# A graph attention kernel: the row writes issued from ScalarE's DMA queue

## The chip, the cores and the metric

The kernel runs on one core of a Trainium2 chip. A core has five engines, each with an instruction stream of its own that is worked through in order: TensorE (PE), VectorE (DVE), ScalarE (ACT), GpSimd (POOL) and SyncE (SP). Data moves between HBM and the core's memory by DMA; a DMA is an instruction in the stream of the engine that issues it, here SP's nearly always and ACT's for a few weights at the start. The metric is the time of one execution on the device, in microseconds (us), as the median of several runs.

## The reference

Two graph attention blocks are applied to 64 graphs of 256 nodes with 512 features each, in float32. In each block the input goes through a layer norm and a ReLU, the attention network is applied, and the result is added to the input:

```python
def gat_layer(x, mask, W, a_src, a_dst, bias, concat):
    xl = (x @ W).reshape(B, N, H, F)
    asrc = jnp.einsum('bnhf,hf->bnh', xl, a_src)
    adst = jnp.einsum('bnhf,hf->bnh', xl, a_dst)
    e = jax.nn.leaky_relu(asrc[:, :, None, :] + adst[:, None, :, :], NEG_SLOPE)
    e = jnp.where(mask[..., None], e, NEG_INF)
    attn = jax.nn.softmax(e, axis=1)
    out = jnp.einsum('bsdh,bshf->bdhf', attn, xl)
    ...
    return out + bias
```

The first block has two such layers: layer 1 with four heads of 256 features and an ELU after it, and layer 2 with one head of 512. The second block has one attention layer of the same kind, called layer 3 here: eight heads of 64 features, the softmax over the other index, and a ReLU on the output.

## The kernel before, in words

Every graph is worked on as two halves of 128 nodes (`T` = 2, `P` = 128 partitions). The work on three graphs is interleaved: a round of the list `order` has steps of the graph whose layer 3 ends (-2), of the one in layers 2 and 3 (-1), of the one in layers 1 and 2 (0), and of the next one, which is loaded and projected (1). Rounds r = 1 to 63 run through `order`; a list `head` stands before them and `tail` after. The lists are written out by hand, and the program does not reorder them: each step appends its instructions to the streams of the engines in the order of the list. So the order within one engine's stream is that of the list.

Projections are matrix products by Strassen's scheme in the class `Product`: seven products p1 to p7, of which four add onto one PSUM tile `sum`, and in between ACT copies the sum's state away (`kept`, L60). PE can only add the next product onto `sum` once ACT has made the copy. `m1a` and `m1b` are the two halves of layer 1's projection, `m2` and `m3` those of layers 2 and 3; what they give is added up by DVE (L260) or copied by ACT (L258).

The softmax is without a maximum: exponentials of the nodes' terms are taken once per node (`exp1`, `exp2`, `exp3`; ACT at L284 and L481), and an edge is the larger of two products of these. For that one factor is needed along the partitions and the other along the free axis. The step that brings it there is `spread` (called by `rows1`, `rows2` and `rows3`, once each per graph):

- DVE transposes 32x32 blocks of the exponentials into `wt` (L237);
- a DMA of 16 KB writes them to a DRAM tile `kept4`, `kept1` or `kept8` (L239);
- one to four DMAs read this tile back, broadcast to all 128 partitions (`bc`, L244). Four are for layer 3, one for layer 2, two for layer 1. They wait until the write has landed.

For the last graph, layers 2 and 3 use the tensor engine instead. The edges (`weigh`) are then two instructions for each half of a head: ACT scales the row (`wy`, L289; three buffers) and DVE takes the larger and applies the mask (`e`, L290). `gat1`, `gat2` and `gat3` (L394, L448, L500) multiply the edges with the features on PE, and `out1`, `out2`, `out3` bring the result out on DVE. After layer 2 come the statistics of the norm (DVE L173 to L179, GpSimd L181 and L183), the norm (ACT L189) and its transpose on PE (`turn3`, L196).

The part of `order` around the three uses of `spread`:

```python
    -1 exp3, -1 rows3, 1 turn1, 0 m2 p6, 0 m2 p5, 0 m2 p7, ...
    0 exp2, 0 rows2, 1 m1a p6, -1 edges3 0, -1 edges3 1, 1 m1b p1, 1 m1a p7, ...
    ... -1 edges3 3, 1 m1a p4, 1 m1b p2, 1 exp1, 1 rows1, -1
    edges3 6, 1 m1b p6, 1 m1b p5
```

After that the next round begins with `edges3 7`, `gat3 0 0`, `edges3 5`, `gat3 0 1`, `edges2`, `m1b p7`, `out3`, `gat2 0`.

A second path with a general softmax is in the program and is entered only when an exponential runs out of range; it does nothing on these inputs.

Of the kernel before, what the change touches and what calls it, by code (L numbers as in the profile page):

```python
# [97 lines left out]
def short_path(ctx, tc, flags, x, adj, w1, att_src1, att_dst1, b1, w2, att_src2, att_dst2, b2, w_proj, w_att,  # L98
               b_att, out):

    nc = tc.nc
# [131 lines left out]
    def spread(w, heads):  # L233


        wt = small.tile([P, 32], F32, name="wt")
        nc.vector.transpose(wt, w)  # L237
        kept = dram.tile([4, 32, 32], F32, name=f"kept{heads}")
        nc.sync.dma_start(kept.rearrange("j c i -> (j c) i"), wt)  # L239
        rows = []  # L240
        for h in range(0, heads, 2):
            k = min(2, heads)
            bc = work.tile([P, 4, T * k, 32], F32, name=f"bc{k}", bufs=3 * k - 2)
            nc.sync.dma_start(bc.rearrange("p j c i -> p j (c i)"),  # L244
                              kept[:, T * h:T * (h + k), :].rearrange("j c i -> j (c i)")[None].to_broadcast([P, 4, 32 * T * k]))
            rows += [bc[:, :, T * i:T * (i + 1), :].rearrange("p j t i -> p t j i") for i in range(k)]
        return rows
# [44 lines left out]
    class Graph:  # L292
# [87 lines left out]
        def rows1(self):  # L380
            self.bc1 = spread(self.w[0], H1)
# [48 lines left out]
        def rows2(self):  # L430
            self.bc2 = None if self.b == B - 1 else spread(self.w[1], 1)
# [51 lines left out]
        def rows3(self):  # L483
            self.bc3 = None if self.b == B - 1 else spread(self.w[2], H3)
# [27 lines left out]
        def range(self):  # L512
            nc.vector.tensor_reduce(ends[:, 0, self.b:self.b + 1], self.exs, AX.X, ALU.max)
            nc.vector.tensor_reduce(ends[:, 1, self.b:self.b + 1], self.exs, AX.X, ALU.min)
# [434 lines left out]
```

## Time and profile before

| | |
|---|---|
| Time, median of 3 runs | 3218.84 us (3214.32 to 3219.35) |
| Profiled execution | 3218.9 us, of which the span from first to last instruction is 3217.2 us |
| PE busy, of the span | 97% |
| DVE, ACT, POOL busy | 71%, 60%, 37% |
| Granted clock of PE, mean | 0.993 |
| Row writes (L239) | 190, 16 KB each, all issued from SP, 1.4 us to landing |
| Broadcast reads of rows (L244) | 380 of 256 KB (5.7 us to landing) and 63 of 128 KB (4.8 us) |

The profile is one execution of the program. A busy share is the time in which an engine executed something. In the timeline each line has the start, the duration, the engine, the source line, the operation, the tiles written and read, and in brackets how long the engine had idled before and what ended that; lines of one kind that follow each other are merged (x3). SPq and ACTq are instructions that the engine's sequencer works on itself, such as the issue of a DMA. A list of waits has the total in us, the number of times and the longest.

### The profile page before, as it was taken

The numbers are of one execution on the slowest core, as the hardware profiler recorded it, in microseconds if no ns is written. First come the engines' busy times: TensorE is split into PE (matmuls) and PEld (weight loads), VectorE is DVE, ScalarE is ACT, GpSimd is POOL, SyncE is SP. The second block draws the span as 40 slices with busy tenths as digits, with TensorE's granted clock in tenths as the row PEclk, the third lists the DMA queues.
The fourth block names the chain that finished last, engine by engine and source line by source line (L and its number), as shares of the span: only waits on it lengthen the run. The fifth ranks groups of instructions, "written<-read, shape, count | busy, mean of one in ns | idle before, by whom it ended". The sixth has DMA issues, their size and how long they took to land. (4 is left out here: it accounts for less than half of the span.)

```text
span 3217.2 us, 60904 instructions
## 1 busy us (share of the span) xinstructions
PE 3133.7 (97%) x21808; PEld 2670.7 (83%) x21808; DVE 2282.5 (71%) x6379; ACT 1917.4 (60%) x4867; POOL 1179.1 (37%) x1434
## 2 busy tenths in 40 slices
PE   4999999999999999999999999999999999999997
PEld 3788888888888888888888888888888888888886
DVE  7667677677677677676676776776776776776765
ACT  2456566656666665665565566566666666655654
POOL 2343343333433433433433433434434334334332
PEclk8999999999999999999999999999999999999999
DMA  4233333333333333333333333332333333333331
GB/s 143 57 95 83 89 88 91 83 91 87 89 87 92 88 86 84 96 81 90 97 80 90 88 89 83 91 92 83 92 87 88 88 91 88 81 89 96 81 90 35
DMA packets 439842, 281.49 MB, mean 87 GB/s; under 512 B 109168, under 2 KB 389744, under 8 KB 439536
## 3 DMA queue, kind: packets, MB, share of 16 engines
q1 hardware_dynamic: 438160, 275.43, 31.9%
q8 instruction: 177, 2.90, 0.4%
q10 hardware_dynamic: 1376, 2.10, 0.2%
q14 instruction: 129, 1.06, 0.1%
HBM read 199.36 MB, written 69.70 MB: 84 GB/s over the span
## 5 line engine op out<-in xcount | busy, mean ns | idle before, releaser
L289 ACT ACTIVATE wy<-bc,exs_sb 128x256 f32<-128x256 f32 x1646 | 706.9, 498 | 176.1 <-DMA bc<-kept 129.3
L260 DVE TENSOR_TENSOR xl<-pm,kept 128x256 f32<-128x256 f32 (+2 forms) x768 | 321.5, 419 | 285.8 <-PE pm L54 208.7
L510 POOL TENSOR_TENSOR x<-x,o 128x256 f32<-128x256 f32 x256 | 181.1, 728 | 916.0 <-DVE r L506 884.4
L394 PE MATMUL pm<-xl,e 128*128 128x257 f32 x2048 | 489.9, 386 | 17.6 <-DVE e L290 13.6
L290 DVE SCALAR_TENSOR_TENSOR e<-wy,exs_sb,cap 128x256 f32<-128x256 f32 x1024 | 435.8, 478 | 92.4 <-ACT wy L289 92.4
L54 PE MATMUL sum<-w_sb,h1s 128*128 128x257 f32 x2048 | 489.0, 381 | 9.3 <-POOL h1s L216 7.0
L60 ACT ACTIVATE kept<-sum 128x264 f32<-128x264 f32 (+3 forms) x768 | 276.5, 376 | 341.9 <-PE sum L54 336.6
L54 PEld LDWEIGHTS sum<-w_sb,h1s 128*128 128x128 f32 x2048 | 389.3, 190 | 68.7 <-POOL h1s L216 7.2
L394 PEld LDWEIGHTS pm<-xl,e 128*128 128x128 f32 x2048 | 374.3, 190 | 84.0 <-DVE e L290 14.9
L54 PE MATMUL pm<-w_sb,h1s 128*128 128x257 f32 x1536 | 371.1, 383 | 10.4 <-DVE xl L260 6.5
L54 PEld LDWEIGHTS pm<-w_sb,h1s 128*128 128x128 f32 x1536 | 287.0, 190 | 74.9 <-POOL hs L216 20.1
L181 POOL TENSOR_TENSOR rstd<-ve,neg_half 128x2 f32<-128x2 f32 x128 | 117.6, 919 | 630.3 <-DVE ve L179 630.3
L500 PEld LDWEIGHTS pm<-xl,e 128*64 128x64 f32 x8192 | 251.0, 138 | 45.4 <-DVE e L290 23.4
L54 PE MATMUL sum<-w1a_sb,hs 128*128 128x260 f32 x1024 | 269.6, 386 | 11.7 <-ACT kept L60 4.5
L290 DVE SCALAR_TENSOR_TENSOR e<-wy,exs_sb,mask 128x256 f32<-128x256 f32 x640 | 270.3, 480 | 13.1 <-ACT wy L289 12.8
L54 PE MATMUL sum<-w1b_sb,hs 128*128 128x256 f32 x1024 | 271.9, 388 | 2.9 <-ACT hs L353 1.5
L500 PE MATMUL pm<-xl,e 128*64 128x65 f32 x8192 | 270.1, 224 | 2.1 <-DVE e L290 1.3
L54 PE MATMUL sum<-wp_sb,hs 128*128 128x264 f32 x1024 | 270.8, 387 | 1.3 <-ACT kept L60 1.1
L407 ACT ACTIVATE ez<-z 128x512 f32<-128x512 f32 x256 | 159.6, 623 | 178.5 <-DVE z L404 178.5
L404 DVE SCALAR_TENSOR_TENSOR z<-pm,r,b_sb 128x256 f32<-128x256 f32 x512 | 247.8, 484 | 18.3
L448 PE MATMUL pm<-xl,e 128*128 128x257 f32 (+1 forms) x1024 | 242.9, 380 | 1.1 <-DVE e L290 1.1
L54 PEld LDWEIGHTS sum<-w1a_sb,hs 128*128 128x128 f32 x1024 | 191.4, 190 | 50.2 <-issue 15.2
(99 smaller groups left out, 5013.4 us busy)
## 6 DMA issues: line engine op xcount, KB each, us to landing
bc<-kept SPq DMA_DIRECT2D x380, 256.0 KB, 5.7
xs<-in_x_dram SPq DMA_DIRECT2D x64, 512.0 KB, 3.9
out_dram<-x SPq DMA_DIRECT2D x64, 512.0 KB, 2.8
kept_h<-h SPq DMA_DIRECT2D x63, 512.0 KB, 3.2
h<-kept_h SPq DMA_DIRECT2D x63, 512.0 KB, 3.7
ad<-in_adj_dram SPq DMA_DIRECT2D x64, 256.0 KB, 4.3
bc<-kept SPq DMA_DIRECT2D x63, 128.0 KB, 4.8
kept<-wt SPq DMA_DIRECT2D x190, 16.0 KB, 1.4
```

What stands on the lines that cost most here:

```text
L54: self.nc.tensor.matmul(to[:, :self.n], self.lhs[:, i, c, :], self.rhs[:, i, c, :], start=(first and c == 0), stop=(last and c == self.nk ...
L60: self.nc.scalar.activation(s[:, :self.n], self.sum[:, :self.n], AF.Copy)
L181: nc.gpsimd.tensor_tensor(rstd, ve[:, 0, :], neg_half, ALU.pow)
L260: nc.vector.tensor_tensor(dst, pm, add, ALU.add)
L289: nc.scalar.activation(wy.rearrange("p (t j i) -> p t j i", t=T, j=4), bc, AF.Copy, scale=yw)
L290: nc.vector.scalar_tensor_tensor(dst, wy, xw, mask, ALU.max, op)
L394: nc.tensor.matmul(pm[:, :Q + 1], self.e[1, h][:, s, t * P:(t + 1) * P], xl1[:, s, h, L1:], start=(s == 0), stop=(s == T - 1))
L404: nc.vector.scalar_tensor_tensor(z[:, sl], pm[:, :Q], r, b1_sb[:, sl], ALU.mult, ALU.add)
L407: nc.scalar.activation(ez, z[:, 2 * g * F1:2 * (g + 1) * F1], AF.Relu, scale=-1.0)
L448: nc.tensor.matmul(pm[:, :n], self.e[2][:, s, t * P:(t + 1) * P], xl2[:, s, half, L2:L2 + n], start=(s == 0), stop=(s == T - 1))
L500: nc.tensor.matmul(pv[q:q + 64, h, :], self.e[3, a * G + h][:, s, t * P + q:t * P + q + 64], xl3[:, s, a * G + h, :], start=(s == 0), stop ...
L510: nc.gpsimd.tensor_tensor(to, to, o.rearrange("p h k -> p (h k)"), ALU.add)
```

## The change

The write of the transposed row to DRAM is issued by ScalarE instead of SyncE. Nothing else is changed. It applies to all three uses, rows1, rows2 and rows3, and to 190 DMAs in the program. In ACT's stream the write stands right behind the three exponentials of its layer and ahead of the instruction that followed them: a copy of `sum` (L60) after layers 2 and 3, and the `wy` of edges3 6 (L289) after layer 1. In SP's stream the reads of `bc` now follow what stood ahead of the write. The streams of PE, DVE and GpSimd are the same as before.

```diff
@@ -236,7 +236,7 @@
         wt = small.tile([P, 32], F32, name="wt")
         nc.vector.transpose(wt, w)
         kept = dram.tile([4, 32, 32], F32, name=f"kept{heads}")
-        nc.sync.dma_start(kept.rearrange("j c i -> (j c) i"), wt)
+        nc.scalar.dma_start(kept.rearrange("j c i -> (j c) i"), wt)
         rows = []
         for h in range(0, heads, 2):
             k = min(2, heads)
```

## The prediction

> **What bounds the kernel now.** I read the page's first part, then windows over one steady graph, SP's own waits, and last the timelines around the three row writes.
>
> The page's first part (engine, busy us, share of the span):
>
> ```profile
> PE 3133.7 (97%) x21808; PEld 2670.7 (83%) x21808; DVE 2282.5 (71%) x6379; ACT 1917.4 (60%) x4867; POOL 1179.1 (37%) x1434
> ```
>
> TensorE is the bound. Busy time by windows in the steady part:
>
> ```profile
> 1000.00:1048.85 48.85, 48.70 (x345) 41.78 (x344) 34.94 (x97) 30.20 (x77) 18.17 (x22) 1.00 0.31 89
> ...
> 1036.00:1048.00 12.00, 12.00 (x111) 10.22 (x109) 11.40 (x36) 6.55 (x14) 3.25 (x6) 1.00 0.36 106
> ```
>
> The columns are length, PE, PEld, DVE, ACT, POOL. A graph takes about 48.85 us and PE is busy 48.70 of it, at full clock (1.00). PE has no slack, so whatever makes it wait is added to the time. ACT has 18 us free per graph, but what counts is whether it is free where its results are due. In the second window DVE is busy 11.40 of 12.00 us: there it can hardly catch up.
>
> SP's waits (total us, times, longest):
>
> ```profile
> SPq L239 <- DVE wt L237: 560.9, 129, 23.7
> SPq L239 <- DVE e L290: 331.6, 61, 5.9
> ...
> SPq L244 <- DMA kept<-wt: 214.7, 190, 2.9
> ```
>
> SP stands 892 us at the row write until VectorE has transposed the row. SP has nothing else to do, so that cost nothing. After the change somebody else stands there. The three places in one graph, in the timeline (start, us, engine, line). First the rows of layer 1, the last of the three:
>
> ```profile
> 1030.13 0.44 ACT L284 ACTIVATE exs_sb<-xl 128x8 f32<-128x8 f32 x3
> ...
> 1030.48 0.89 ACT L289 ACTIVATE wy<-bc,exs_sb 128x256 f32<-128x256 f32 x2
> ...
> 1031.05 0.20 DVE L237 STREAM_TRANSPOSE wt<-exs_sb 128x32 f32<-128x32 f32 x1
> ...
> 1031.28 0.33 SPq L239 DMA_DIRECT2D kept<-wt  x1
> ...
> 1031.57 0.38 ACT L60 ACTIVATE kept<-sum 128x256 f32<-128x256 f32 x1 [0.20 <-PE sum L54]
> 1031.85 2.49 ACT L289 ACTIVATE wy<-bc,exs_sb 128x256 f32<-128x256 f32 x6
> ...
> 1033.98 0.88 DVE L290 SCALAR_TENSOR_TENSOR e<-wy,exs_sb,mask 128x256 f32<-128x256 f32 x2
> ```
>
> ACT finishes the exponentials at 1030.57, but DVE reaches the transpose only at 1031.05, behind its queue of edges; SP issues at 1031.28. ACT meanwhile goes on with eight wy. Second, the row of layer 2:
>
> ```profile
> 1023.96 0.44 ACT L284 ACTIVATE exs_sb<-xl 128x2 f32<-128x2 f32 x3
> ...
> 1024.43 0.33 SPq L239 DMA_DIRECT2D kept<-wt  x1
> 1024.55 0.39 ACT L60 ACTIVATE kept<-sum 128x260 f32<-128x260 f32 x1 [0.16 <-PE sum L54]
> ...
> 1025.22 0.60 PE L54 MATMUL sum<-w1a_sb,hs 128*128 128x260 f32 x2
> ```
>
> The matmuls at 1025.22 add onto the sum which the copy (L60) must have read; it is read by 1024.94. Third, the point where the chain comes back to PE (turn3):
>
> ```profile
> 1046.49 1.52 ACT L189 ACTIVATE h<-x,off,rstd 128x512 f32<-128x512 f32 x2 [0.78 <-POOL off L183]
> ...
> 1048.06 0.31 PEld L196 LDWEIGHTS pt<-ident,h 128*128 128x128 f32 x3 [0.16 <-ACT h L189]
> ```
>
> h is ready at 1048.01 and the weight load starts 0.05 us later, having waited 0.16; the matmuls over it (1047.97 on) just lose nothing. The chain DVE, GpSimd, ACT into turn3 has no slack left.
>
> **What the Trainium skill says.** "DMA: Bandwidth & Descriptors", section "Issuing engines are not separate DMA queues": transfers from any engine run on the same 16 DMA engines, and another issuer saves only sequencer time. So the 16 KB write itself gains nothing; its landing stays 1.4 us in this trace. "Perfetto Trace Analysis", section "DMA Instruction — HWDGE (DVE, Sync)": the sequencer itself does the semaphore wait and the descriptor generation, and is free for the next instruction only at the end of the profiled window. The section "DVE / Act Engine Instruction (TENSOR_ADD, Activation, etc)" there says that an ACTIVATE's wait sits in a queue beside the sequencer. So a waiting DMA holds up every later ACTIVATE. The trace agrees as far as it goes: at the start two ACT issues run from 12.38 to 14.12 and the next ACTIVATE starts at 14.17, 0.05 after. The skill's section "SWDGE vs HWDGE vs iDMA" of the DMA page says that an issue from ACT is of the same kind as one from SP; here a 256 KB w1a issue takes 374 ns on ACT and 368 on SP, so I take SP's 0.33 us for the kept write on ACT.
>
> **The change part by part.** All 190 writes (64 of layer 1, 63 each of layers 2 and 3) leave SP and come into ACT's stream right behind the exponentials. On PE, DVE and GpSimd no instruction moves. On SP the next instruction is the bc load, which waits for the write to land (1.4 us) as before; 0.33 us of SP's issue per write is saved on an idle queue: nothing.
>
> *Layer 3's row.* DVE has the row transposed at 1015.41 and ACT's last exponential ends at 1015.64, so ACT does not wait; it issues until 1015.97 at the latest, and the copy behind it (1015.55 before) runs from 1016.02 to 1016.39. The sum that it reads is wanted by PE at 1016.99, and ACT's next copy idles 3.0 us for PE. Cost 0; these 0.6 us on PE's side are the cover. Without them: 0.3 to 0.5 us each.
>
> *Layer 2's row.* DVE is quick here (transposed at 1024.40), so ACT issues 1024.43 to 1024.76, the copy starts at 1024.81 instead of 1024.55 and ends at 1025.20. In this graph PE starts 0.14 us after such a release (at 1019.92, after DVE's 1019.78) and the first eight matmuls then take 1.98 instead of 1.90. So PE goes on at 1025.34 instead of 1025.22: 0.12 + 0.08 = 0.20 us. In 16 of 61 steady graphs the records have PE itself over 0.05 us later at this sum, which hides part of the delay; I take 0.16 on average.
>
> *Layer 1's rows.* ACT waits until 1031.28, issues to 1031.61, goes on at 1031.66 instead of 1030.48: 1.18 us late. Queued behind: two wy, the copy, six wy, whose consumers are DVE's edges. The wy start 0.40 apart, so the copy would have been ready at 1031.28 but waited for PE until 1031.57: 0.29 comes back. The last wy ends 0.89 late, and so do the layer 2 edges (L290 with mask, 1034.86 to 1035.75), as DVE was waiting for ACT. PE's gat2 loads its first edge weights at 1035.10 and wants the first half, now at 1035.35: 0.3 us of stall. DVE stays 0.89 late through out3 and out2; at the second L458 it had been waiting for PE (1036.65 to 1037.73 for two, where 0.88 is needed): 0.20 comes back. From there to the statistics of layer 3 DVE has no gap, so h reaches turn3 0.89 - 0.20 = 0.69 us late against a slack of zero. PE's total per graph is the 0.69 (the 0.3 at gat2 lies within it), on top of layer 2's 0.16.
>
> *Sum.* The place occurs in the 62 rounds that have a next graph: 62 x (0.69 + 0.16) = 53 us, and about 2 for refilling PE after a stall. The head's writes are covered (ACT idles 9.0 us there for bc). Profiled execution: 3218.9 (span 3217.2) + 55 = 3274. The median of the runs is 3218.84, the same, so I forecast 3273.
>
> *Ends of the unknown price.* No row shows an ACT issue in the steady part. If it took ACT no time and only the wait counted: layer 2 nothing, layer 1 0.85 - 0.29 - 0.20 = 0.36, 22 us. At the longest ACT issue of the trace (0.545): 0.2 more at both places, 1.27 per graph, 79 us. Below nothing is excluded for ACT's part: no work leaves it.
>
> **The rivals.**
> Absorbed further on (+7 to +30 us, about 3237): DVE or ACT finds slack before turn3 that I haven't seen. For: ACT idles 1.82 us for bc later in the round. Against: it is DVE that is late then, and DVE is full.
> Unchanged (3219): a waiting DMA doesn't hold up the ACTIVATEs behind it. For: the trace has no ACT issue that waits for DVE. Against: the order at the start.
> Faster (3201 at best): on a ring of its own the row write lands earlier, bc arrives earlier, and ACT's waits for bc (129.3 us in 54) shrink. PE idles 5.6 us in 1000, so all its stalls are worth 18 us. It decides only if the write's 1.4 us falls by more than ACT's 1.18 us of delay; nothing queues ahead of the write on SP's ring at those moments.
> A larger loss (above +80, about 3315): the late DVE also holds PSUM buffers which gat2 and gat1 want, and the stalls add up instead of lying within each other.
>
> **How the numbers follow.** The forecast 0.65; absorbed 0.16; larger 0.09; unchanged 0.06; faster 0.04. A measurement tells about 0.2% (6.4 us) from no change. Slower is 0.65 + 0.16 + 0.09 = 0.90, same 0.06, faster 0.04. The range from +18 to +87, 3237 to 3306, holds the forecast case with both ends of the issue's price, half of the absorbed case and a little of the larger one, about 8 in 10.
>
> **What would show it.** In the changed profile: the kept write as an ACT issue of about 0.33 us; the period at 49.7 us; ACT idle some 0.7 to 1.1 us before wy in each graph with the DMA issue in it; DVE waiting longer for ACT's wy; new waits of PE's weight loads for DVE's e at L448 and for ACT's h at L196, and of PE's sum for ACT's L60. I am wrong if ACT's next instruction starts before the write's issue has ended, if h at turn3 is no later against PE than now, or if the bc loads land more than 0.3 us earlier.

## The result, and the profile after

| | before | after |
|---|---|---|
| Time, median (runs side by side on one chip, 4 each) | 3216.58 us (3213.99 to 3219.35) | 3259.88 us (3257.87 to 3260.22) |
| Ratio, 95% interval | | 1.0133 (1.0120 to 1.0145) |
| Span of the profiled execution | 3217.2 us | 3258.3 us |
| Granted clock of PE, mean | 0.993 | 0.993 |
| Row writes, issue | 332 ns on SP | 326 ns on ACT |
| Row writes, to landing | 1.4 us | 1.4 us |
| Start of one gat2 to the next, median of the steady rounds | 48.58 us | 49.36 us |

The change costs 43.3 us, 0.70 us for each of the 62 rounds that have a next graph. The forecast was 3273, 54 us more. The writes are no cheaper from ACT, and no earlier: in the median a row of layer 1 lands 1.45 us after its transposing has ended, before 1.44. The median round grew by 0.78 us, more than the 0.70 that the times give; where the difference goes is told under "Absorbed further on".

The page's first part for the changed kernel (engine, busy us, share of the span, instructions):

```profile
PE 3178.6 (98%) x21808; PEld 2651.7 (81%) x21808; DVE 2280.4 (70%) x6379; ACT 1929.8 (59%) x4867; POOL 1179.6 (36%) x1434
```

Its busy time by windows, the first from gat2 to gat2 (length, then PE, PEld, DVE, ACT, POOL):

```profile
1047.34:1096.70 49.36, 49.21 (x341) 41.08 (x340) 34.92 (x98) 30.09 (x76) 18.18 (x22) 1.00 0.30 88
```

A reader who looks for idle time of PE finds none: its busy time *grew* by 44.9 us with the same 21808 matmuls, and it is busy 49.21 of 49.36 us. In these records the time in which matmuls wait lies inside the matmuls: eight of them at gat2 take 2.22 us where they took 1.89, as shown below. The loss shows in three other places: in the period, in the busy share of the weight loads (81% of the span, 83% before), and in the mean length of one matmul. The group of gat2's matmuls, page of before and then of after (total us, mean ns of one):

```profile
L448 PE MATMUL pm<-xl,e 128*128 128x257 f32 (+1 forms) x1024 | 242.9, 380 | 1.1 <-DVE e L290 1.1
```

```profile
L448 PE MATMUL pm<-xl,e 128*128 128x257 f32 (+1 forms) x1024 | 264.4, 392 | 1.5 <-DVE e L290 1.1
```

The waits of the changed kernel (engine, what it wanted, from whom; total us, times, longest):

```profile
DVE e L290 <- ACT wy L289: 158.0, 192, 4.2
ACT wy L289 <- DVE wt L237: 67.2, 62, 1.1
PEld pm L448 <- PE pm L448: 22.6, 62, 0.7
PEld pm L448 <- DVE e L290: 21.9, 63, 1.5
PEld pm L394 <- issue: 20.0, 59, 0.4
PEld pt L196 <- ACT h L189: 15.5, 66, 2.3
```

ACT now stands 1.08 us (67.2 / 62) in every round at the instruction behind the write. DVE waits for ACT's wy 158.0 us (105.2 before). Weight loads of gat2 wait for DVE's edges 63 times (once before), and for gat2's own matmuls 62 times. Loads of gat1 (L394) waited 10.8 us before. The wait for h at turn3 (L196) is the same 15.5 us in 66 as before.

The rows of layer 1 in the timeline, ACT and then DVE (start, us, in brackets the idle time before and what ended it):

```profile
1042.07 0.44 ACT L284 ACTIVATE exs_sb<-xl 128x8 f32<-128x8 f32 x3
1043.22 0.33 ACTq L239 DMA_DIRECT2D kept<-wt  x1
1043.60 0.91 ACT L289 ACTIVATE wy<-bc,exs_sb 128x256 f32<-128x256 f32 x2 [1.08 <-DVE wt L237]
1044.41 0.36 ACT L60 ACTIVATE kept<-sum 128x256 f32<-128x256 f32 x1
```

```profile
1042.99 0.20 DVE L237 STREAM_TRANSPOSE wt<-exs_sb 128x32 f32<-128x32 f32 x1
1044.14 0.89 DVE L290 SCALAR_TENSOR_TENSOR e<-wy,exs_sb,cap 128x256 f32<-128x256 f32 x2 [0.95 <-ACT wy L289]
```

The exponentials end at 1042.51, the transposed row is there at 1043.19, the issue runs from 1043.22 to 1043.55, and wy starts 0.05 us later. Before, wy started 0.35 us after the first exponential, now 1.53. The copy (L60) follows wy at once; before it had waited for PE. DVE, which had no gap there before, now waits 0.95 us.

The row of layer 2 in a round where PE doesn't come late itself:

```profile
1134.43 0.44 ACT L284 ACTIVATE exs_sb<-xl 128x2 f32<-128x2 f32 x3
...
1134.90 0.33 ACTq L239 DMA_DIRECT2D kept<-wt  x1
1135.28 0.39 ACT L60 ACTIVATE kept<-sum 128x260 f32<-128x260 f32 x1 [0.41 <-PE sum L54]
...
1135.78 0.74 PEld L54 LDWEIGHTS sum<-w1a_sb,hs 128*128 128x128 f32 x4 [0.33 <-issue]
```

The copy starts 0.85 us after the first exponential (0.59 before) and ends at 1135.67; PE's next weight load starts 0.11 later and has waited 0.33 (0.08 in the median before). The view names no releaser here, but the load starts 0.11 us after the end of this copy in both kernels, whenever the copy comes.

Where PE takes the delay of layer 1, first at gat2. The eight matmuls before:

```profile
1035.31 1.89 PE L448 MATMUL pm<-xl,e 128*128 128x257 f32 x8
```

And after, with the edges and the load ahead of them:

```profile
1046.81 0.88 DVE L290 SCALAR_TENSOR_TENSOR e<-wy,exs_sb,mask 128x256 f32<-128x256 f32 x2
...
1047.34 0.73 PEld L448 LDWEIGHTS pm<-xl,e 128*128 128x128 f32 x4 [0.33 <-DVE e L290]
1047.34 2.22 PE L448 MATMUL pm<-xl,e 128*128 128x257 f32 x8
```

The first half of the edges is there at about 1047.29, the load starts 0.05 later, and the eight matmuls take 2.22 us where they took 1.89. Then at gat1, ahead of turn3. Before:

```profile
1045.59 0.42 DVE L508 SCALAR_TENSOR_TENSOR o<-pm,r 128x256 f32<-128x256 f32 x1
...
1046.13 0.51 PEld L394 LDWEIGHTS pm<-xl,e 128*128 128x128 f32 x3 [0.19 <-issue]
```

After:

```profile
1058.13 0.42 DVE L508 SCALAR_TENSOR_TENSOR o<-pm,r 128x256 f32<-128x256 f32 x1
...
1058.67 0.95 PEld L394 LDWEIGHTS pm<-xl,e 128*128 128x128 f32 x5 [0.34 <-issue]
...
1060.51 1.08 PE L196 MATMUL pt<-ident,h 128*128 128x128 f32 x8
1060.60 0.75 PEld L196 LDWEIGHTS pt<-ident,h 128*128 128x128 f32 x7 [0.17 <-ACT h L189]
```

DVE's o (L508) reads a PSUM buffer (`pm`, of which there are four) until 1058.55, and 0.12 us after that a weight load of gat1 starts. In the kernel before it was the same 0.12 (1046.01, then 1046.13), but the load had waited 0.19 instead of 0.34. The view again names no releaser; what ties the load to this o is that the 0.12 stands in each of the 61 steady rounds (those with the same list of instructions), before and after. At turn3 the load has waited 0.17, against 0.16 before.

### The profile page after: what moved, and what is told of

Read it like the earlier page. It is cut to its first block, busy times and chain, and to the rows that moved or that the text cites. A ratio compares the mean times of both kernels' runs of the same rounds, so it can differ in the third digit from the quotient of the medians.

```text
span 3258.3 us, 60780 instructions
## 1 busy us (share of the span) xinstructions
PE 3178.6 (98%) x21808; PEld 2651.7 (81%) x21808; DVE 2280.4 (70%) x6379; ACT 1929.8 (59%) x4867; POOL 1179.6 (36%) x1434
## 5 line engine op out<-in xcount | busy, mean ns | idle before, releaser
L289 ACT ACTIVATE wy<-bc,exs_sb 128x256 f32<-128x256 f32 x1646 | 710.3, 499 | 262.0 <-DMA bc<-kept 114.8
L290 DVE SCALAR_TENSOR_TENSOR e<-wy,exs_sb,cap 128x256 f32<-128x256 f32 x1024 | 439.1, 482 | 151.3 <-ACT wy L289 151.3
L394 PE MATMUL pm<-xl,e 128*128 128x257 f32 x2048 | 497.9, 387 | 13.6 <-DVE e L290 12.7
L394 PEld LDWEIGHTS pm<-xl,e 128*128 128x128 f32 x2048 | 375.5, 191 | 86.3 <-issue 20.0
L60 ACT ACTIVATE kept<-sum 128x264 f32<-128x264 f32 (+3 forms) x768 | 277.1, 377 | 277.6 <-PE sum L54 261.6
L290 DVE SCALAR_TENSOR_TENSOR e<-wy,exs_sb,mask 128x256 f32<-128x256 f32 x640 | 269.4, 479 | 6.8 <-ACT wy L289 6.8
L448 PE MATMUL pm<-xl,e 128*128 128x257 f32 (+1 forms) x1024 | 264.4, 392 | 1.5 <-DVE e L290 1.1
L448 PEld LDWEIGHTS pm<-xl,e 128*128 128x128 f32 x1024 | 181.9, 190 | 68.9 <-PE pm L448 22.6
```

The lines of the kernel that those rows point to most:

```text
L60: self.nc.scalar.activation(s[:, :self.n], self.sum[:, :self.n], AF.Copy)
L289: nc.scalar.activation(wy.rearrange("p (t j i) -> p t j i", t=T, j=4), bc, AF.Copy, scale=yw)
L290: nc.vector.scalar_tensor_tensor(dst, wy, xw, mask, ALU.max, op)
L394: nc.tensor.matmul(pm[:, :Q + 1], self.e[1, h][:, s, t * P:(t + 1) * P], xl1[:, s, h, L1:], start=(s == 0), stop=(s == T - 1))
L448: nc.tensor.matmul(pm[:, :n], self.e[2][:, s, t * P:(t + 1) * P], xl2[:, s, half, L2:L2 + n], start=(s == 0), stop=(s == T - 1))
```

## The experiments

All were timed in five rounds beside the kernel before on the same chip; its medians there were 3215.14 (rows apart, late), 3213.27 (wait alone, twice, GpSimd, early) and 3215.34 us (layer 2 late). Lines of kernel.py stand one to five further down where an edit adds some. Theory A in the expectations is the prediction's chain with its sizes taken from the changed kernel's profile; the other letters are its rivals, as each expectation says them. "Per graph" is the difference of the medians over 62.

**Each row alone.** One edit, three kernels:

```diff
-    def spread(w, heads):
+    def spread(w, heads, by=nc.sync):
...
-        nc.sync.dma_start(kept.rearrange("j c i -> (j c) i"), wt)
+        by.dma_start(kept.rearrange("j c i -> (j c) i"), wt)
...
-            self.bc1 = spread(self.w[0], H1)
+            self.bc1 = spread(self.w[0], H1, nc.scalar)
```

The second has nc.scalar at layer 2's call, the third at layer 3's.

> Only layer 1's row write is issued from ACT, layers 2 and 3 stay on SP. Theory A (ACT stands at the write until DVE has transposed, and everything behind it is late): this row carries most of the loss, 62 x (0.50 to 0.69) = +31 to +43 us against the kernel before; ACT idles about 1.1 us before the wy behind the write. Rival B (each issue from ACT costs alike, 43 us / 190 = 0.23 us, for the engine's time in it or for the other ring): 64 x 0.23 = +15 us.

> Only layer 2's row write is issued from ACT. Theory A: no wait, since DVE is ready when ACT arrives; the issue alone delays the copy of the sum by 0.26 us and PE by 0.15 on average: 62 x 0.15 = +9 us (+5 to +13). Rival B: 63 x 0.23 = +14 us.

> Only layer 3's row write is issued from ACT. Theory A: the issue falls into ACT's 3 us of idle time and the sum is wanted 0.6 us later: 0 us (-4 to +4). Rival B: 63 x 0.23 = +14 us.

Layer 1's rows: 3250.60 us, ratio 1.0108 (1.0092 to 1.0123), +35.5. Layer 2's: 3224.43, 1.0030 (1.0019 to 1.0042), +9.3. Layer 3's: 3214.11, 0.9998 (0.9990 to 1.0007), -1.0. The sum of the three is 43.8, the whole change cost 43.3: the parts add up, and layer 1 is four fifths of it. Per graph 0.57, 0.15 and 0. Rival B, one price for every issue (+15 and twice +14), fails at layers 1 and 3.

Why layer 3 costs nothing, in the timeline of the third kernel:

```profile
1110.10 0.33 ACTq L239 DMA_DIRECT2D kept<-wt  x1
1110.11 0.20 ACT L481 ACTIVATE exs_sb<-lg 128x16 f32<-128x16 f32 x1
1110.48 0.39 ACT L60 ACTIVATE kept<-sum 128x257 f32<-128x257 f32 x1 [0.17 <-issue]
1113.60 0.39 ACT L60 ACTIVATE kept<-sum 128x257 f32<-128x257 f32 x1 [2.74 <-PE sum L54]
```

ACT idles only 0.17 us, as the row was ready and the issue ran beside the last exponential. The copy starts 0.37 us after that exponential instead of 0.10, so it is 0.27 late; the next copy waits 2.74 us for PE anyway (3.02 before).

**Layer 1's write from ACT, but later.** The transposing stays where it was on DVE (a step of its own, flip1), and the write is listed behind the two wy of edges3 6. Of the edit only the part in `order` is shown, abridged:

```diff
-        edges3 2, ... 1 m1b p2, 1 exp1, 1 rows1, -1 edges3 6, 1 m1b p6, 1 m1b p5
+        edges3 2, ... 1 m1b p2, 1 exp1, 1 flip1, -1 edges3 6, 1 rows1, 1 m1b p6, 1 m1b p5
```

> Only layer 1's row write is issued from ACT, and two instructions later in ACT's stream: DVE transposes where it did, ACT first does the two wy of edges3 6, then issues. By then the row is transposed, so the same issue stays and the wait goes. Theory A: ACT issues from about the same moment as SP before, the copy behind it is 0.1 us late where it has 0.29 us of slack: 0 us (-4 to +5). Rival B: as for the first kernel with this row alone, +15 us, or whatever that one shows.

3215.19 us, 0.9999 (0.9991 to 1.0007). The same 64 writes on the same queue cost nothing:

```profile
1027.25 0.90 ACT L294 ACTIVATE wy<-bc,exs_sb 128x256 f32<-128x256 f32 x2
1028.06 0.33 ACTq L244 DMA_DIRECT2D kept<-wt  x1
1028.43 0.38 ACT L60 ACTIVATE kept<-sum 128x256 f32<-128x256 f32 x1 [0.28 <-DVE e L295]
```

wy starts 0.35 us after the first exponential, as before. The issue lies ahead of the copy, where ACT idles 0.28 us; in the kernel before it idled 0.20 there for PE. So it isn't ACT's queue or its ring that costs, but where in ACT's stream the write stands.

**The wait without the issue.** The write stays on SP; ACT copies one column of the row, so that it waits for DVE at the same place, but issues nothing:

```diff
         nc.sync.dma_start(kept.rearrange("j c i -> (j c) i"), wt)
+        if heads == 4:
+            nc.scalar.activation(small.tile([P, 1], F32, name="seen"), wt[:, :1], AF.Copy)
```

> All three writes stay on SP; at layer 1's row ACT gets a copy of one column of the transposed row, so that it waits for DVE as at the write, but issues no DMA. Theory A (standing in the wait is what costs): ACT's next wy starts at about 0.03 + 0.13 us after the transpose, 0.94 us late instead of 1.19; the layer 1 write alone cost 0.57 of its 1.19 us per graph, so 0.62 is absorbed, and 0.94 - 0.62 = 0.32 remains: 62 x 0.32 = +20 us (+13 to +27). Rival C (ACT's DMA issue, or the write on ACT's ring, makes the loss): 0 to +3 us.

3230.65 us, 1.0058 (1.0044 to 1.0072), +17.4:

```profile
1029.69 0.45 ACT L286 ACTIVATE exs_sb<-xl 128x8 f32<-128x8 f32 x3
1030.85 0.20 ACT L241 ACTIVATE seen<-wt 128x1 f32<-128x1 f32 x1 [0.71 <-DVE wt L237]
1030.96 0.89 ACT L291 ACTIVATE wy<-bc,exs_sb 128x256 f32<-128x256 f32 x2
```

A said +20. About half of layer 1's loss comes with the wait alone; the rest is the issue on top of it, which holds ACT for 0.38 us (1043.22 to 1043.60 above) where the small copy holds it for 0.11 (1030.85 to 1030.96): 62 x 0.27 = 17, and 35.5 - 17.4 = 18. The issue costs this because the wait has already used up what slack there is; at the later place above it cost nothing.

**The write twice.** Layer 1's from ACT, followed by a second one to a DRAM tile that nothing reads:

```diff
+        by = nc.scalar if heads == 4 else nc.sync
+        by.dma_start(kept.rearrange("j c i -> (j c) i"), wt)
+        if heads == 4:
+            again = dram.tile([4, 32, 32], F32, name="again")
+            by.dma_start(again.rearrange("j c i -> (j c) i"), wt)
```

> Layer 1's write from ACT as in the run with this row alone (+35.5 us), and behind it a second write of the same row from ACT into a DRAM tile that nobody reads. Theory A: the slack is used up, so every further 0.37 us of ACT (issue and restart) comes out in full: 62 x 0.37 = +23 more, +58 us in all. Rival C: what counts is when the row lands and is read back; the second write comes after the first and nothing waits for it: +35 us as with one.

3280.65 us, 1.0211 (1.0197 to 1.0225), +67.4; A said 58. The step from the single write is 31.9, not 23:

```profile
1046.85 0.33 ACTq L240 DMA_DIRECT2D kept<-wt  x1
1047.22 0.44 ACTq L243 DMA_DIRECT2D again<-wt  x1
1047.71 0.91 ACT L293 ACTIVATE wy<-bc,exs_sb 128x256 f32<-128x256 f32 x2 [1.56 <-DVE wt L237]
```

The second issue right behind the first took 444 ns in the median (327 to 936), not 326. wy started 2.01 us after the first exponential, 0.48 later than with one write, and 62 x 0.48 = 30. That fits A's chain; its price for the second issue was wrong.

**The write earlier.** Layer 1's from ACT, and the exponentials and the transposing listed ahead of m1b p2, so that DVE is quicker at it:

```diff
-        edges3 2, ... 1 m1a p4, 1 m1b p2, 1 exp1, 1 rows1, -1 edges3 6, ...
+        edges3 2, ... 1 m1a p4, 1 exp1, 1 rows1, 1 m1b p2, -1 edges3 6, ...
```

> Layer 1's write from ACT at its place behind the exponentials, but the steps exp1 and rows1 stand before m1b p2 in the list, so that DVE transposes one instruction (0.34 to 0.42 us) earlier, ahead of the sum of m1b p2. Theory A: ACT waits 0.3 instead of 0.7 us and is 0.78 us late instead of 1.19; 0.78 - 0.62 = 0.16 remains: 62 x 0.16 = +10 us (0 to +16). Rival B (the issue costs, not the wait): +35 us as without the shift.

3222.61 us, 1.0028 (1.0017 to 1.0040), +9.3 instead of +35.5; A said +10:

```profile
1028.70 0.44 ACT L285 ACTIVATE exs_sb<-xl 128x8 f32<-128x8 f32 x3
1029.44 0.33 ACTq L240 DMA_DIRECT2D kept<-wt  x1
1029.81 0.91 ACT L290 ACTIVATE wy<-bc,exs_sb 128x256 f32<-128x256 f32 x2 [0.67 <-DVE xl L261]
```

wy starts 1.11 us after the first exponential instead of 1.53. Together with the kernel before these give a curve:

| layer 1's write | wy behind the first exponential | later than before | lost per graph | later, less what was lost |
|---|---|---|---|---|
| on SP (before), or late on ACT | 0.35 us | 0 | 0 | |
| early on ACT | 1.11 | 0.76 | 0.15 | 0.61 |
| on SP, ACT waits only | 1.27 | 0.92 | 0.28 | 0.64 |
| on ACT | 1.53 | 1.18 | 0.57 | 0.61 |
| on ACT, twice | 2.01 | 1.66 | 1.09 | 0.57 |

(Medians of the rounds, that of the third row from the lines above.) The four kernels in which ACT is late lie on one line: about 0.6 us of the delay cost nothing, and what is beyond is lost at the full rate. No kernel had a delay between 0 and 0.76 us, so the flat part is drawn from that line and not measured.

**The write from GpSimd.** Layer 1's only, `by = nc.gpsimd if heads == 4 else nc.sync`.

> Layer 1's row write is issued from GpSimd, the others from SP. Theory A: the loss comes from what is queued behind the wait, and behind this one on GpSimd stands nothing until out3 (GpSimd idles 14 us up to there): 0 us (-4 to +5), unless the write from GpSimd lands over 0.7 us later than from SP, when the layer 1 edges would be late: up to +20. Rival D (any engine but SP at this place costs the same as ACT): +35 us.

3221.45 us, 1.0026 (1.0016 to 1.0035), +8.2. The timeline of GpSimd:

```profile
1032.06 0.63 POOL L240 DMA_DIRECT2D kept<-wt  x1 [9.50 <-DVE wt L237]
1036.10 1.41 POOL L511 TENSOR_TENSOR x<-x,o 128x256 f32<-128x256 f32 x2 [3.40 <-DVE r L507]
```

GpSimd has 9.50 us to wait in and 3.40 to spare behind, so neither the wait nor the issue (629 ns, nearly twice ACT's) holds up anything behind it, and D's +35 didn't come. It is not free, though: A's 0 (-4 to +5) missed. The row lands 2.08 us after its transposing has ended, 0.64 later than from SP (1.44), which is just under the 0.7 that A had named as the point from which layer 1's edges would be late; whether that costs the 8.2 us isn't shown. The median period is 48.65 us in this profile (48.58 before) and the mean 48.79 (48.80). 42.0 us follow the start of the last gat2 instead of 39.5, but that stretch is also 40.9 us with layer 1's write late and 37.9 with layer 2's late, which cost next to nothing. So the cause of the 8.2 us stays open.

**Layer 2's write later.** Layer 2's only, from ACT, listed behind the copy that follows it, with the transposing left in place:

```diff
-        0 exp2, 0 rows2, 1 m1a p6, -1 edges3 0, ...
+        0 exp2, 0 flip2, 1 m1a p6, 0 rows2, -1 edges3 0, ...
```

> Only layer 2's row write is issued from ACT, one instruction later: behind the copy of m1a p6's sum instead of ahead of it (DVE transposes where it did). Theory A: PE gets that copy in time, but the four wy and the copy of m1a p7 behind the write are now 0.37 us late; DVE's c22 waits for that copy and PE's m1a p3 for c22, which had next to no slack (it ended 0.15 us before the matmul). So the stall moves instead of going: 0.2 to 0.35 us per graph, +12 to +22 us, no better than the +9.3 us of the write ahead of the copy. Rival E (only the copy of m1a p6 matters; whatever else ACT delays has room): 0 us (-4 to +4).

3217.62 us, 1.0006 (0.9998 to 1.0014), +2.3. A missed and E holds: A had wy 0.37 us late.

```profile
1024.26 0.39 ACT L60 ACTIVATE kept<-sum 128x260 f32<-128x260 f32 x1 [0.16 <-PE sum L54]
1024.32 0.33 ACTq L244 DMA_DIRECT2D kept<-wt  x1
1024.69 1.71 ACT L294 ACTIVATE wy<-bc,exs_sb 128x256 f32<-128x256 f32 x4
```

The sequencer issues from 1024.32 to 1024.65, *while* the copy runs from 1024.26 to 1024.65: the copy had been handed to the engine, and the row had been ready since 1024.10. wy starts 0.43 us after the copy instead of the usual 0.28, so only 0.15 of the issue is paid. This is how the Trainium skill has it ("Perfetto Trace Analysis", section "Sequencer Loop"): engine instructions are pushed into a queue, while a control instruction starts executing in the sequencer's own microcode; the trace fits if an issue is of the second kind. Behind a running ACTIVATE 0.23 of the 0.38 us are hidden here; the 0.33 + 0.05 us in full are paid where ACT stands empty, as it does at layer 1.

## Why the prediction was right

**The writes themselves.** Issue price taken from SP, 0.33 us: measured 326 ns, and the restart of 0.05 us also. Landing unchanged. Two rivals fall: "unchanged" (a waiting DMA doesn't hold up the ACTIVATEs) with the 67.2 us of waits at wy and the 35.5 us of layer 1's row; "faster" with the landing of 1.4 us. ACT's waits for bc went from 129.3 to 114.8 us, but they are 104.6 us with layer 3's row alone and 100.9 with layer 1's write late, so this total says nothing about the change.

**Layer 3's row = 0.** Right, -1.0 us, with an interval that holds no change.

**Layer 2's row = 0.16.** Right: 0.15 per graph. The copy came 0.26 late as worked out. In the records PE's matmuls at this sum lose about 0.20 in 44 of 61 steady rounds, and in the others PE is late by itself; with this row alone the median round is 0.19 longer (48.77 us).

**Layer 1's rows = 0.69.** The way from ACT over DVE to PE was right up to gat2; the size was 0.57 by the times and 0.59 in the median round (49.17 us with this row alone). Taken one by one: wy 1.18 late, right to the hundredth. 0.29 back at the copy, right (the copy follows wy without a wait now). The edges of layer 2 0.89 late: 0.88 in the median of the records of DVE over the steady rounds, each taken from its transposing on. gat2 stalls 0.3: PE's matmuls there lose about 0.41. 0.20 comes back at the second L458: right, from 0.86 to 0.66; that pair of DVE instructions, before and after, stands

```profile
1036.65 1.08 DVE L458 SCALAR_TENSOR_TENSOR x<-pm,r,xs 128x256 f32<-128x256 f32 x2
1049.45 0.88 DVE L458 SCALAR_TENSOR_TENSOR x<-pm,r,xs 128x256 f32<-128x256 f32 x2
```

back to back now (0.88 us where it was 1.08). What failed is the step "From there to the statistics of layer 3 DVE has no gap": it has small ones. DVE makes up 0.02 to 0.03 just ahead of that pair and 0.05 to 0.06 ahead of the edges (L290) that follow the next L458, where before it had started 0.04 us ahead of the recorded end of its predecessor and now starts 0.08 ahead. They take the lateness to 0.60, and in the median it stays there until the row of layer 2. The table of delays says the same from the times: 1.18 less the 0.6 that cost nothing is 0.58.

**"h reaches turn3 0.69 late against a slack of zero."** Wrong as to the place, and by one of the signs that the prediction itself had set: h is later, but not against PE, which is already as late by then. L196 waits the same 15.5 us. PE had taken the second part of the loss a little earlier, at gat1 (0.15 per graph in the records, and L394's waits from 10.8 to 20.0 us), waiting, as the constant 0.12 us says, for the buffer which the late o of DVE was still reading. That is the mechanism of the rival "a larger loss", PSUM buffers held by the late DVE; only its claim that the stalls add up is wrong. gat2's 0.41, 0.03 at m1b p3 and 0.15 at gat1 make 0.59, which is DVE's whole lateness and no more. So the total didn't suffer from the wrong place: PE had no slack against the late DVE at gat1 either. The prediction hadn't looked there, and that part was luck.

**"2 for refilling PE".** Not there: 62 x (0.57 + 0.15) is 44.6, and the change cost 43.3.

**"Absorbed further on".** A little, and where this rival had put it: at ACT's wait for bc later in the round. Of the 0.85 per graph worked out, the median round shows 0.78 (0.59 and 0.19) and the times 0.70. Before, DVE stood at the first edges of layer 1 (L290), waiting for ACT's wy, in 10 of the 61 steady rounds, 5.9 us in all; in 7 of them ACT had just waited for bc. A late DVE has nothing to wait for there, and so loses less: after the change it is 3 rounds and 0.7 us. 62 x 0.78 - 5.2 = 43 us, as measured. How often bc comes late there differs from profile to profile with nothing changed in the median, however (2.3 us with layer 3's row alone, 4.5 with layer 1's write late), so the size of this part is uncertain.

The period was forecast at 49.7 us and is 49.36 in the median (before 48.58, not the 48.85 of the round that was shown).

## What to carry to other kernels

On ACT a DMA that had to wait for another engine held up what stood behind it in the stream: before moving one to a computing engine, look at when its input is ready and at what stands behind it, not at how busy the engine is. ACT was idle 40% of the time before the change and the move still cost 1.3%, 1.1% of it for layer 1's write, while this same write two instructions further down ACT's stream cost nothing. On SP, whose only work here is issuing, 892 us of waiting were free, and there was nothing to gain.

## What the runs showed of the hardware

- Two issues in a row on ACT: the second 16 KB write took 444 ns in the median, the first 326.
- An issue whose wait is met when the sequencer reaches it runs beside the ACTIVATE ahead of it: of 0.38 us only 0.15 were paid at layer 2's late write, 0.27 at layer 3's.
- An issue of the same write from GpSimd took 629 ns, and the row landed 0.64 us later than from SP. The move of 64 writes cost 8.2 us that neither GpSimd's wait nor its issue explains.
- PE's lost time showed as longer matmuls (380 to 392 ns in the mean at L448, 44.9 us more busy time in all), not as idle PE.
